# A two-layer convolution block: the order of stores, loads and projections in its first stage, and buffers for its last pieces

## The chip, the cores and the metric

The kernel runs on one core of a Trainium2 chip. The metric is the device time of one execution in microseconds, from the first to the last instruction. All data are float32.

A core has a matrix engine (TensorE), which writes its results into the accumulator memory PSUM; a vector engine (VectorE); a scalar engine (ScalarE), which applies functions and scales; and GpSimd. Each of them works through its own queue of instructions in order. Transfers between the chip's main memory and the on-chip memory are issued here by SyncE (SP in the profile), which does nothing else, by GpSimd (POOL), and at the very end by ScalarE. An issue waits in its queue until what it depends on is done, and everything behind it in that queue waits with it.

## The reference, cut to what matters

The input x has 16 images of 192 channels and 64 by 64 pixels.

```python
# layer 0
h = layernorm_over_channels(x)                     # per pixel
projected, gate = split(conv1x1(h, in_proj))       # 192 -> 2 * 192 channels
projected = depthwise3x3(projected, dw_k)
scanned = weighted sum of four running averages of projected (left, right, down, up)
mixed = (scanned + depthwise3x3(projected, le_k)) * sigmoid(gate)
mixed = gelu(batchnorm(mixed))                     # statistics over all images and pixels
x = x + conv1x1(mixed, out_proj)
x = x + conv1x1(gelu(conv1x1(layernorm(x), fc1)), fc2)   # 192 -> 768 -> 192
# layer 1
t = relu(bn(mean_over_pixels(x) @ w1.T))           # per image
taps = t @ w2.T + b2                               # 3x3 taps per image and channel, masked to 4
out = depthwise3x3(x, taps) + bias
```

The batch norm needs the statistics of all images before its output can be used, so the kernel can't run image by image from end to end.

## The kernel before

Three stages follow each other.

**First stage (L454 to L584): normalise and project.** A pair of images is taken together, one on each half of the 128 partitions. The pixels are cut into n_ac = 64 chunks of 4 groups (AR = 4) of 128 pixels for each of the two images. Four chunks make a block (`per` = 4), and there are 16 blocks. For chunk n:

- `load_a(n)` loads the pixels into one of four xa buffers: six transfers of 128 KB, three on SyncE's queue and three on GpSimd's.
- `turn(n)` transposes them on TensorE into the PSUM tile ps_xt, of which there is one, so that VectorE can take the variance over channels (`variance`, L491 and L492, once for each group). `deviation(n)` takes the root on ScalarE and the reciprocal on VectorE.
- `project(n)` multiplies the raw pixels by the projection weights wi, from which the mean over channels was subtracted (`projection_weights`, in three steps: scale on VectorE, mean on TensorE at L281, subtract on VectorE at L284). Each group fills two PSUM tiles ps_pj, each kept twice. VectorE (L517) and ScalarE (L518) evict one each and multiply it by the reciprocal deviation.
- The evictions write into the block's staging buffer: stg for even blocks, a part of mid for odd ones. So a buffer comes round every second block, and the first eviction of a block waits until the block two before has been stored.

The store of a block is spread over the four iterations of the next block: at its first iteration `store_first` (four transfers of 64 KB) and two parts of `store` (four of 64 KB and four of 448 KB), then one part in each iteration, four transfers of 448, 320 and 192 KB. They lie half on SyncE's queue and half on GpSimd's.

Before the change, iteration n of the loop at L564 puts first `load_a(n + 3)` into the queues, then the stores. The load takes the buffer of chunk n - 1, so it waits for the last matmul of project(n - 1). Then come turn(n + 1), project(n) with the variances of chunk n + 1 among its groups, deviation(n + 1), and the small work that `beside` has set down for this iteration: decay tables, bias rows, their stores to main memory (lv_d, dv_d), and from iteration 40 on the loads of weights and of the first matrices for the second stage (`load_dm`, `load_lm`).

**Second stage: convolution as matrices, scans, gate.** It goes over the channels in 24 groups and reads what the first stage stored. The change leaves it alone.

**Third stage: the rest of layer 0, and layer 1.** It goes over n_ch = 64 chunks of 512 pixels of each image of a pair. Layer 1 of a pair (`dynamic`, 12 pieces of 128 by 1024) is spread over the chunks of the next pair. The last pair has no next one; its twelve pieces come at the end, in `dynamic_last`, in the order of L1109 to L1121. Five of them are done by ScalarE (first tap, L1029) and VectorE (the other three taps, L65 called from L1031). Seven are done on TensorE with the taps on diagonals of small matrices (L1038) and evicted by ScalarE (L1040). All twelve take their output buffer from the ring gl, which has four buffers and was also used by the hidden layer.

The order of instructions on every engine is the order of the program text.

Of the kernel before, what the change touches and what calls it, by code (L numbers as in the profile page):

```python
# [21 lines left out]
F32 = mybir.dt.float32  # L22
# [6 lines left out]
HW = 64  # L29
NPIX = HW * HW  # L30
RW = HW + 2
CH = 512
# [3 lines left out]
GR = 2 * CR  # L36
# [8 lines left out]
AR = CR // 2  # L45
# [10 lines left out]
def conv_block_kernel(ctx: ExitStack, tc: tile.TileContext, x, prm, w_in, w_out, w_fc1, b_fc1, w_fc2, w1, bn1, w2, out):  # L56
# [189 lines left out]
    with ExitStack() as stage:  # L246
# [8 lines left out]
        dg = cut(64, 768, 576).rearrange("p (t k n) -> p t k n", t=3, k=3)  # L255
# [16 lines left out]
        def projection_weights():  # L272

            by_group = lambda v: v.rearrange("p (k g c) -> p g k c", k=2, c=GC)
            flat = lambda v: v.rearrange("p g k c -> p (g k c)")
            for t in range(3):
                nc.vector.tensor_scalar_mul(wi[:, t], by_group(w0[:, t]), pt3[:, t, LN1W:LN1W + 1])
            yield
            pc = bank()
            for t in range(3):  # L280
                nc.tensor.matmul(pc[:, 0:2 * C], mean_w, flat(wi[lo, t]), start=(t == 0), stop=(t == 2))  # L281
            yield
            for t in range(3):
                nc.vector.tensor_sub(flat(wi[:, t]), flat(wi[:, t]), pc[:, 0:2 * C])  # L284
            yield

        def decays():

            nc.scalar.activation(dec, pt3[lo, :, DEC:DEC + 4], AF.Sigmoid)
            nc.vector.tensor_scalar(dec, dec, 0.05, 0.995, ALU.max, ALU.min)  # L290
            nc.scalar.activation(tmp, pt3[lo, :, ISC:ISC + 4], AF.Tanh)
            nc.vector.tensor_scalar_add(tmp, tmp, 1.0)
            nc.vector.tensor_reduce(red, pt3[lo, :, MIX:MIX + 4], AX.X, ALU.max)
            for t in range(3):
                nc.vector.tensor_scalar(gain[:, t], pt3[lo, t, MIX:MIX + 4], red[:, t:t + 1], None, ALU.subtract)
            nc.scalar.activation(gain, gain, AF.Exp)
# [125 lines left out]
        def beside(n, f, *args):  # L422
            side.setdefault(n, []).append((f, args))
# [21 lines left out]
                beside(end + 1 + part, store_vector, k, part)  # L445
        for k in (0, 1, 3, 4):
            beside(40 + k, load_weights, k)
        beside(46, load_dm, 0)
        beside(47, load_lm, 0)
        beside(48, load_dm, 1)  # L450
        beside(49, load_lm, 1)
        beside(50, squeeze_scale)

        xp = stage.enter_context(tc.tile_pool(name="xa", bufs=4))  # L454
# [4 lines left out]
        n_ac = n_pairs * NCH  # L459
# [4 lines left out]
        stag = {}  # L464

        def load_a(n):
            blk, part = divmod(n, per)
            p, u = divmod(blk, 2)
            xa = xp.tile([128, 3, CH], F32, tag="xa", name="xa")
            for i, q in enumerate(HALF):  # L470
                for t in range(3):
                    (nc.sync, nc.gpsimd)[i].dma_start(  # L472
                        xa[q, t].rearrange("p (g n) -> p g n", n=128), xr[2 * p + i, u, :, t, part * AR:(part + 1) * AR])
            ast[n]["xa"] = xa

        def pixels(n, t, g):
            return ast[n]["xa"][:, t, g * 128:(g + 1) * 128]

        def turn(n):

            xt = psa.tile([128, 3, AR, 128], F32, tag="xt", name="ps_xt")
            for t in range(3):
                for g in range(AR):
                    nc.tensor.transpose(xt[:, t, g], pixels(n, t, g), ident)  # L484
            ast[n].update(xt=xt, st6=sp.tile([128, AR, 2, 6], F32, tag="st6", name="st6"),
                          mv=sp.tile([128, AR, 2, 2], F32, tag="mva", name="mva"))

        def variance(n, g):
            s = ast[n]
            for i, q in enumerate(HALF):  # L490
                nc.vector.bn_stats(s["st6"][:, g, i], s["xt"][:, :, g, q])  # L491
                nc.vector.bn_aggr(s["mv"][:, g, i], s["st6"][:, g, i])  # L492

        def deviation(n):
            rs = sp.tile([128, AR, 2], F32, tag="rsa", name="rsa")
            nc.scalar.activation(rs, ast[n]["mv"][:, :, :, 1], AF.Sqrt, bias=eps6)
            nc.vector.reciprocal(rs, rs)
            ast[n]["rs"] = rs

        def project(n):  # L500
            blk, part = divmod(n, per)
            if part == 0:
                if blk % 2:
                    both_i = mid.rearrange("p (i o j) -> p i o j", i=2, j=BR)
                else:
                    both_i = stg.tile([128, 2, 2 * C, BR], F32, tag="stg", name="stg")
                stag[blk] = [both_i[:, i] for i in range(2)]
            for g in range(AR):
                ps = [psa.tile([128, 2 * C], F32, tag=f"pj{i}", name=f"ps_pj{i}", bufs=2) for i in range(2)]
                for t in range(3):  # L510
                    for i, q in enumerate(HALF):
                        nc.tensor.matmul(ps[i], pixels(n, t, g)[q], wi[q, t].rearrange("p g k c -> p (g k c)"),  # L512
                                         start=(t == 0), stop=(t == 2))
                if n + 1 < n_ac:
                    variance(n + 1, g)
                j, rs = part * AR + g, ast[n]["rs"]
                nc.vector.tensor_scalar_mul(stag[blk][0][:, :, j], ps[0], rs[:, g, 0:1])  # L517
                nc.scalar.activation(stag[blk][1][:, :, j], ps[1], AF.Copy, scale=rs[:, g, 1:2])  # L518
# [21 lines left out]
        for dst, src in ((pt3, prm), (w0, w_in)):  # L540
            v = src.rearrange("(t p) n -> p t n", p=64)
# [12 lines left out]
        steps = projection_weights()  # L554
        next(steps)
        decays()
        turn(0)
        next(steps)
        for g in range(AR):
            variance(0, g)  # L560
        next(steps)
        deviation(0)

        for n in range(n_ac):  # L564
            if n + 3 < n_ac:
                load_a(n + 3)
            blk, part = divmod(n, per)
            if blk:
                if part == 0:
                    store_first(blk - 1)  # L570
                    store(blk - 1, 0, (nc.gpsimd, nc.sync))
                store(blk - 1, part + 1, (nc.gpsimd, nc.sync))
                if part == per - 1:
                    stag.pop(blk - 1)
            if n + 1 < n_ac:
                turn(n + 1)
            project(n)
            if n + 1 < n_ac:
                deviation(n + 1)
            for f, args in side.pop(n, ()):  # L580
                f(*args)
# [5 lines left out]
    with ExitStack() as stage:  # L587
# [163 lines left out]
        for k in range(-2, n_bp + 1):  # L751
            if 0 <= k + 1 < n_bp:
                tables(k + 1)
            if k >= 1:
                vertical(k - 1)
                gate(k - 1)
                g, c = divmod(k, hp_)
# [57 lines left out]
    hp2 = ctx.enter_context(tc.tile_pool(name="h2", bufs=2))  # L815
    wp = ctx.enter_context(tc.tile_pool(name="w2", bufs=1))
    op = ctx.enter_context(tc.tile_pool(name="o2", bufs=2))
# [202 lines left out]
    def dynamic_last(p, g, t, dg, queues=(nc.gpsimd, nc.sync)):  # L1020

        xi, taps, r = ximg[p % n_img], pst[p]["taps"], g * GR
        o = wp.tile([128, GR, HW], F32, tag="gl", name="ol", bufs=4)
        src = lambda k, r0, nr: xi[:, t, r0 + k // 3:r0 + k // 3 + nr, k % 3:k % 3 + HW]
        if dg is None:
            for k in range(NTAP):
                w = taps[:, t, k:k + 1]
                if k == 0:
                    nc.scalar.activation(o, src(k, r, GR), AF.Identity, bias=pt3[:, t, BIAS:BIAS + 1], scale=w)  # L1029
                else:  # L1030
                    stt(o, src(k, r, GR), w, o)  # L1031
        else:

            ps = ps2.tile([128, 2, CH], F32, tag="f1", name="ps_d", bufs=2)
            for k in range(NTAP):
                for i, q in enumerate(HALF):
                    for h in range(2):
                        nc.tensor.matmul(rows(ps[HALF[h], i]), dg[q, k, q], src(k, r + h * CR, CR)[q],  # L1038
                                         start=(k == 0), stop=(k == NTAP - 1))
            nc.scalar.activation(o.rearrange("p h w -> p (h w)"), ps.rearrange("p k n -> p (k n)"), AF.Identity,  # L1040
                                 bias=pt3[:, t, BIAS:BIAS + 1])
        for i in range(2):
            if dg is None:
                nc.sync.dma_start(ov[2 * p + i, 64 * t:64 * t + 64, r * HW:(r + GR) * HW], o[HALF[i]].rearrange("p h w -> p (h w)"))
            for h in range(2 if dg is not None else 0):
                r0 = r + h * CR
                queues[h].dma_start(ov[2 * p + i, 64 * t:64 * t + 64, r0 * HW:(r0 + CR) * HW],
                                                  o[HALF[h], i * CR:(i + 1) * CR].rearrange("p h w -> p (h w)"))
# [115 lines left out]
```

## Time and profile before

| | us |
|---|---|
| time, median of 3 runs (lowest to highest) | 3752.0 (3748.82 to 3752.39) |
| span of the profiled execution | 3750.8 |
| TensorE busy | 3696.1 |
| VectorE busy | 2716.6 |
| ScalarE busy | 1794.8 |
| GpSimd busy | 420.2 |
| first matmul of project(0) | 21.93 |
| last matmul of project(63) ends | 633.5 |
| second stage, about | 640 to 1360 |
| taps of the last pair are there, the twelve pieces begin | 3714.85 |

The profile page gives busy times and counts, then the span in 40 equal slices of 94 us, where a digit is the busy share in tenths. A line of the timeline has the start, the duration, engine and line, operation, out<-in with shapes, and in brackets the idle time of the engine before it and what ended that. What ended it is inferred: where several transfers land close together, another of them may be named. On SyncE a line's duration is the time in which its queue was held by the issue.

### The profile page before, as it was taken

Reading aid. Unit: us, or ns where it says so; the run is one execution under the profiler, and the core shown is the slowest. Engines: PE = TensorE matmul, PEld = TensorE weight load, DVE = VectorE, ACT = ScalarE, POOL = GpSimd, SP = SyncE. Lnnn points to the kernel's source line nnn. Section 1 sums busy time; section 2 is a strip of 40 time slices with the busy share of each in tenths; the row PEclk is TensorE's granted clock in tenths of the full one; section 3 lists DMA queues with packets and bytes.
Section 4 is the critical chain, followed back from the end, with each engine's and each line's share of the span. In section 5 each row is a group of like instructions: output and inputs, shape, how many; then the busy total and the mean of one; then the engine's idle time right before and its main releaser. Section 6 shows DMA issues by size and latency. Waiting matters only on the chain.

```text
span 3750.8 us, 71230 instructions
## 1 busy us (share of the span) xinstructions
PE 3696.1 (99%) x30252; PEld 1651.4 (44%) x30252; DVE 2716.6 (72%) x4260; ACT 1794.8 (48%) x1945; POOL 420.2 (11%) x683
## 2 busy tenths in 40 slices
PE   8999999999999979999999999999999999999998
PEld 5666666555555533333333333333333333333333
DVE  6887776999999965557756766666766776675763
ACT  3443434888888833334443434443443434443432
POOL 2334332101001020000000000000000000000000
PEclk9999999999999989999999999999999999999999
DMA  6899998999999950112222222222222221221212
GB/s 163 241 251 235 269 283 249 294 281 277 274 283 269 242 104 18 56 39 71 72 62 66 62 68 64 67 57 68 76 61 55 78 71 40 80 76 43 68 37 74
DMA packets 308429, 491.76 MB, mean 131 GB/s; under 512 B 46656, under 2 KB 202640, under 8 KB 308112
## 3 DMA queue, kind: packets, MB, share of 16 engines
q1 hardware_dynamic: 250064, 295.14, 29.7%
q0 software_dynamic: 57152, 190.94, 18.9%
q8 instruction: 239, 3.92, 0.5%
q10 hardware_dynamic: 896, 1.12, 0.1%
q14 instruction: 78, 0.64, 0.1%
HBM read 284.91 MB, written 197.92 MB: 129 GB/s over the span
## 4 chain that ended last, share of the span: by engine, by line
PE 97%; DVE 1%; DMA 1%; ACT 0%; issue 0%; SPq 0%; ACTq 0%; POOL 0%; DVEq 0%
PE ps_f L955 27%; PE ps_f L828 26%; PE ps_pj L512 13%; PE ps_l L662 11%; PE ps_d L618 7%; PE ps_o L887 5%; PE ps_xt L484 2%; PE ps_o L883 2%; PE ps_o L916 2%; DMA xa<-in_x_dram 1%; PE ps_k L828 0%; DVE v L653 0%; DVE v L655 0%; DMA out_dram<-ol 0%; PE ps_d L1038 0%
## 5 line engine op out<-in xcount | busy, mean ns | idle before, releaser
L957 ACT ACTIVATE gl<-ps_f,bf 128x1024 f32<-128x1024 f32 x384 | 427.6, 1114 | 1316.3 <-PE ps_f L955 1316.3
L955 PE MATMUL ps_f<-h,wf 64*64 64x512 f32 x9216 | 1035.9, 595 | 6.8 <-DVE h L943 6.7
L828 PE MATMUL ps_f<-gl,place 128*64 128x512 f32 x4608 | 1022.2, 592 | 0.0
L955 PEld LDWEIGHTS ps_f<-h,wf 64*64 64x64 f32 x9216 | 334.5, 133 | 693.8 <-issue 642.6
L828 PEld LDWEIGHTS ps_f<-gl,place 128*64 128x64 f32 x4608 | 334.2, 137 | 574.5 <-issue 533.4
L512 PE MATMUL ps_pj<-wi,xa 64*128 64x384 f32 x3072 | 513.8, 487 | 4.0 <-DVE stg L517 3.9
L923 DVE TENSOR_TENSOR h<-ximg,ps_o 128x768 f32<-128x768 f32 x128 | 116.4, 951 | 425.5 <-PE ps_o L887 417.2
L512 PEld LDWEIGHTS ps_pj<-wi,xa 64*128 64x128 f32 x3072 | 292.2, 187 | 197.7 <-issue 10.7
L893 DVE SCALAR_TENSOR_TENSOR ximg<-ps_o,pt,low 128x256 f32<-128x256 f32 x384 | 168.0, 480 | 267.5 <-PE ps_o L887 264.9
L65 DVE SCALAR_TENSOR_TENSOR o<-ximg,taps,o 128x1024 f32<-128x1024 f32 x252 | 323.2, 1282 | 8.7 <-ACT o L1014 2.6
L1018 POOL DMA_DIRECT2D out_dram<-o x168 | 87.9, 528 | 2067.6 <-DVE o L65 2064.8
L942 DVE RECIPROCAL rs<-rs 128x512 f32<-128x512 f32 x64 | 214.3, 3349 | 27.0 <-ACT rs L939 27.0
L653 DVE TENSOR_TENSOR_SCAN v<-tab,q 128x1024 f32<-128x1024 f32 x96 | 218.3, 2274 | 7.8 <-ACT tab L641 7.8
L655 DVE TENSOR_TENSOR_SCAN v<-tab,q 128x1024 f32<-128x1024 f32 x96 | 217.5, 2265 | 0.0
L887 PE MATMUL ps_o<-low,wo 128*64 128x256 f32 x1536 | 210.2, 395 | 0.0
L518 ACT ACTIVATE stg<-ps_pj,rsa 128x384 f32<-128x384 f32 x128 | 119.8, 940 | 187.9 <-PE ps_pj L512 177.0
L641 ACT ACTIVATE tab<-mask,dec_b 128x1024 f32<-128x1024 f32 x192 | 209.0, 1137 | 0.0
L518 ACT ACTIVATE mid<-ps_pj,rsa 128x384 f32<-128x384 f32 x128 | 120.6, 943 | 181.6 <-PE ps_pj L512 175.0
L491 DVE BATCH_NORM_STATS2 st<-ps_xt 128x6 f32<-128x192 f32 x512 | 173.2, 338 | 17.1 <-PE ps_xt L484 16.9
L239 DVE STREAM_TRANSPOSE low<-low 128x512 f32<-128x512 f32 x174 | 167.6, 1014 | 2.1 <-issue 0.3
L975 DVE SCALAR_TENSOR_TENSOR ximg<-ps_f,pt,ximg 128x512 f32<-128x512 f32 x192 | 134.4, 749 | 40.2 <-PE ps_f L828 37.8
L472 POOL DMA_DIRECT2D xa<-in_x_dram x192 | 119.8, 630 | 357.8 <-PE ps_pj L512 279.3
(197 smaller groups left out, 4101.9 us busy)
## 6 DMA issues: line engine op xcount, KB each, us to landing
low<-in_x_dram SPq DMA_DIRECT2D x128, 384.0 KB
out_dram<-o POOLq DMA_DIRECT2D x168, 256.0 KB, 3.7
mid<-pg_d SPq DMA_DIRECT2D x8, 4096.0 KB
low<-mixed_d SPq DMA_DIRECT2D x116, 256.0 KB
low<-pg_d SPq DMA_DIRECT2D x7, 4096.0 KB
pg_o<-pg_d SPq DMA_DIRECT2D x7, 4096.0 KB
xa<-in_x_dram POOLq DMA_DIRECT2D x192, 128.0 KB, 5.9
xa<-in_x_dram SPq DMA_DIRECT2D x192, 128.0 KB
```

The lines of the kernel that those rows point to most:

```text
L65: nc.vector.scalar_tensor_tensor(o, in0, scalar, in1, ALU.mult, ALU.add, **kw)
L512: nc.tensor.matmul(ps[i], pixels(n, t, g)[q], wi[q, t].rearrange("p g k c -> p (g k c)"), start=(t == 0), stop=(t == 2))
L518: nc.scalar.activation(stag[blk][1][:, :, j], ps[1], AF.Copy, scale=rs[:, g, 1:2])
L618: nc.tensor.matmul(dst(ps[o, ih]), mats[g % 2]["dm"][q, di + 1, :, ch], src(s["pg"][q, :, 0, ch]), start=(di == 0), stop=stop)
L653: nc.vector.tensor_tensor_scan(vf, tab, q, 0.0, ALU.mult, ALU.add)
L655: nc.vector.tensor_tensor_scan(vf[:, ::-1], tab[:, ::-1], q[:, ::-1], 0.0, ALU.mult, ALU.add)
L662: nc.tensor.matmul(dst(bst[k]["ps"][i][o]), lm_of(g)[q, m, :, c], src(q, ih), start=start, stop=stop)
L828: nc.tensor.matmul(ps[q], w(i), rhs(i), start=start, stop=stop)
L887: nc.tensor.matmul(ps[q, wh].rearrange("p (r w) -> p r w", w=32), wo[:, 64 * t:64 * t + 64], cols(rows(s["mx"][:, i]))[:, :, wh], start=Fa ...
L942: nc.vector.reciprocal(rs, rs)
L955: nc.tensor.matmul(pf[o, i], wf1[q, t, m0:m0 + 64], s["h"][q, t], start=(t == 0), stop=(t == 2))
L957: nc.scalar.activation(gl, pf, AF.Gelu, bias=bf1[:, m:m + 1])
```

## The change

There are four edits.

1. **Stores ahead of the load.** In iteration n the stores of the block before go into the queues first, and `load_a(n + 3)` after them. They are meant to leave as soon as their data is there, and not to stand behind a load that waits for a buffer.
2. **Matrix loads spread.** The four loads of the second stage's first matrices were set down for iterations 46, 47, 48 and 49; now load_dm is at 46 and 50, load_lm at 48 and 52. This is meant to take them out of the way of stores and x loads.
3. **Projection ahead of transposes, at the start.** The three steps of `projection_weights` are done before the first transposes. In iteration 0 the first two groups are projected before turn(1), and the variances of chunk 1 follow two at a time in the other two groups. All later iterations keep their order. TensorE is meant to begin sooner.
4. **Own output buffers for VectorE's pieces at the end.** The five pieces that VectorE does take their output from the ring o (two buffers, for g below 2, three pieces) and from the ring h2 (two buffers, for the other two), both unused by then. The ring gl is left to the seven pieces of TensorE.

```diff
-        beside(46, load_dm, 0)
-        beside(47, load_lm, 0)
-        beside(48, load_dm, 1)
-        beside(49, load_lm, 1)
+        for i in range(2):
+            beside(46 + 4 * i, load_dm, i)
+            beside(48 + 4 * i, load_lm, i)
...
-        def project(n):
+        def project(n, groups, beside_it):
+
             blk, part = divmod(n, per)
-            if part == 0:
+            if blk not in stag:
...
-            for g in range(AR):
+            for g in groups:
...
-                if n + 1 < n_ac:
-                    variance(n + 1, g)
+                for v in beside_it(g) if n + 1 < n_ac else ():
+                    variance(n + 1, v)
...
         decays()
+        next(steps)
+        next(steps)
         turn(0)
-        next(steps)
         for g in range(AR):
             variance(0, g)
-        next(steps)
         deviation(0)
 
         for n in range(n_ac):
-            if n + 3 < n_ac:
-                load_a(n + 3)
             blk, part = divmod(n, per)
             if blk:
...
                 store(blk - 1, part + 1, (nc.gpsimd, nc.sync))
...
+            if n + 3 < n_ac:
+                load_a(n + 3)
+
+            h = AR // 2 if n == 0 else 0
+            project(n, range(h), lambda g: ())
             if n + 1 < n_ac:
                 turn(n + 1)
-            project(n)
+            project(n, range(h, AR), lambda g: (g,) if h == 0 else (2 * (g - h), 2 * (g - h) + 1))
...
     def dynamic_last(p, g, t, dg, queues=(nc.gpsimd, nc.sync)):
...
-        o = wp.tile([128, GR, HW], F32, tag="gl", name="ol", bufs=4)
+        if dg is None:
+            o = (op.tile([128, GR, HW], F32, tag="o", name="o") if g < 2 else
+                 hp2.tile([128, 3, CH], F32, tag="h2", name="ol")[:, 0:2].rearrange("p k (h w) -> p (k h) w", w=HW))
+        else:
+            o = wp.tile([128, GR, HW], F32, tag="gl", name="ol", bufs=4)
```

## The prediction

> **What bounds the kernel now.** I read the page's busy shares first, then TensorE's waits, then the stretches in which TensorE is idle.
>
> ```profile
> PE 3696.1 (99%) x30252; PEld 1651.4 (44%) x30252; DVE 2716.6 (72%) x4260; ACT 1794.8 (48%) x1945; POOL 420.2 (11%) x683
> PE   8999999999999979999999999999999999999998
> DMA  6899998999999950112222222222222221221212
> ```
>
> TensorE is busy for 3696.1 of 3750.8 us, so all its idle time is 54.7 us, and no edit here takes a matmul away. By stretch: 11.85 us lie in the first 20 us, 5.0 in the rest of the first stage, 25.6 between 700 and 1390, 12.4 in the last 51. The third is a stage that VectorE fills (661.4 of 690 us) and that the edits don't touch; it only starts earlier or later. So the change works on about 29 us.
>
> The first stage, by stretch (us, then TensorE, its weight loads, VectorE, ScalarE, GpSimd busy, clock, DMA share, GB/s):
>
> ```profile
> 20.00:270.00 250.00, 249.95 (x1619) 159.09 (x1619) 200.53 (x660) 98.55 (x132) 88.16 (x148) 1.00 0.82 220
> 270.00:560.00 290.00, 286.08 (x1824) 177.92 (x1821) 216.77 (x642) 115.81 (x155) 114.73 (x191) 1.00 0.99 263
> ```
>
> TensorE sets the pace, 9.40 us a chunk, and from 270 to 560 us the DMA engines are full beside it. There it loses 3.92 us, in two stalls (timeline of TensorE, then of ScalarE and SyncE, round the longer one):
>
> ```profile
> 330.54 4.14 PE L512 MATMUL ps_pj<-wi,xa 64*128 64x384 f32 x24
> 337.21 4.14 PE L512 MATMUL ps_pj<-wi,xa 64*128 64x384 f32 x24 [2.54 <-DVE stg L517]
> ```
> ```profile
> 336.18 1.58 ACT L518 ACTIVATE stg<-ps_pj,rsa 128x384 f32<-128x384 f32 x2 [6.13 <-DMA low<-mid]
> ```
> ```profile
> 310.98 11.96 SPq L472 DMA_DIRECT2D xa<-in_x_dram  x3
> 322.98 2.12 SPq L536 DMA_DIRECT2D pg_d<-stg  x2
> 325.27 3.26 SPq L472 DMA_DIRECT2D xa<-in_x_dram  x3
> 328.57 1.25 SPq L536 DMA_DIRECT2D pg_d<-stg  x2
> ```
>
> Chunk 32 opens a block and writes into stg. ScalarE and VectorE wait for a DMA; what holds that buffer is the last store of the block two before. SyncE issued it at 328.57, behind an x load that waits for project of chunk 30 to give its buffer back. TensorE stops once both PSUM buffers are full. The same happens at 488.6 (1.38 us).
>
> The x loads had time to spare (tile xa, issue to landing):
>
> ```profile
> DMA to landing us min/median/max: 3.1/5.9/11.2
> ```
>
> A load issued at the start of iteration n is wanted by turn(n+3), two chunks on, 18.8 us: typically 12.9 us spare.
>
> The end:
>
> ```profile
> 3728.92 1.11 ACT L1040 ACTIVATE ol<-ps_d,pt 128x1024 f32<-128x1024 f32 x1 [2.51 <-DMA out_dram<-ol]
> 3735.77 1.24 ACT L1029 ACTIVATE ol<-ximg,pt,taps 128x1024 f32<-128x1024 f32 x1 [2.99 <-DVE ol L65]
> 3744.62 1.11 ACT L1040 ACTIVATE ol<-ps_d,pt 128x1024 f32<-128x1024 f32 x1 [3.45 <-DMA out_dram<-ol]
> ```
>
> Twelve pieces go through four gl buffers; from the fifth on ScalarE waits until a store has landed.
>
> [...]SyncE's and GpSimd's transfers together give the 0.99. [...]the store stands behind the waiting load. [...]Here twelve transposes take 2.82 us at 19.18 and 1.53 later; if they switched from 3.26 (three fours of 1.09) to 1.53, the switch fell near 21.6, 7.6 us after work became continuous at 14.03. [...]and I use 7.6.
>
> **Part 1, the start.** Before: transposes wait for x until 14.03, the mean matmuls run 15.04 to 19.2 (4.21), turn(1) to 21.9, project(0) from 21.93, project(1) from 31.33.
> After: VectorE has wi at 9.55 (8.47 + 1.08), so the mean matmuls fill the wait: 9.6 to 13.8. turn(0) has its first two thirds of x by then (they started at 11.47 at the latest) and its last at 14.0: three times 1.09, to 17.1. VectorE subtracts by 15.3 (1.48), hidden by turn(0). Two groups of project(0) follow at once, 4.0 us (half of 8.01), to 21.1; their results wait in PSUM. VectorE's variance(0) takes 3.84 (15.15 to 18.99 before), 17.1 to 20.95, so turn(1) may overwrite xt at 21.1 (1.5, to 22.6). The deviation is there at 21.55, and two evictions of 0.9 end at 23.35. Groups 2 and 3 end at 26.6.
> Now VectorE is last: four variances of 1.02 and two evictions of 0.9 from 23.35, with the fourth variance ahead of the last eviction, end the reads of xt at 28.35. turn(2) waits for that, and project(1) starts at 29.9 instead of 31.33: **-1.4 us**. Bounds: -3.1 if VectorE didn't hold turn(2); +2.4 if the first two groups still ran at half rate.
>
> **Part 2, stores ahead of loads, matrix loads spread.** Bytes by the issue sizes: a block of four chunks stores 2.36, 1.83, 1.31 and 0.79 MB in its four iterations and loads 0.79 MB in each: 9.44 MB in 37.6 us, 251 GB/s, where 263 were moved when full. I count 265 and take the DMA as one line, from a block's start:
> - Last store. Before, it can't be issued until 28.2 (its load waits), and the 9.44 MB end at 36; the first write into that buffer comes 2.1 us into the next block at 39.7. Spare: 4 us, which the lag round chunk 32 exceeded by 2.5. After, it goes one chunk sooner and one load fewer lies ahead: 8.65 MB, plus 1.0 for the last eviction, 33.6. Spare: 6.
> - First load. After, it stands behind 2.36 MB and the wait for the last eviction (VectorE ends 30.9 where the matmuls ended 29.9): 3.15 MB are 11.9, plus 1.0, 12.9 of the 18.8 us. Spare: 5.9 instead of 12.9.
> - Second load: 5.77 MB, 21.8 + 1.0 = 22.8, wanted at 28.2. Spare 5.4. The third and fourth have 7 and 10.
> So the smallest spare grows from 4 to 5.4 us, and the load wait that is added (behind it on SyncE and GpSimd are only later stores and small loads; turn waits for it) stays inside it. A lag of 6.5 as round chunk 32 would still leave 1.1 us, but stores issued a chunk sooner fill moments in which the DMA had nothing (share 0.67 and 0.85 from 290 to 298 us: 2 us). Moving three matrix loads one to three iterations later takes 640 KB, 2.5 us, from ahead of the store that stalled at 488.6. I take both stalls as gone, and 0.6 us in which chunk 44 ran long (8.61 for 8.01), less 0.3: **-4.2 us**. Bounds: 0 to -4.5.
>
> **Part 3, the end.** Same instructions, other buffers. VectorE's five pieces leave the gl ring; the seven TensorE pieces have four buffers of their own. Up to 3726.4 nothing changes (VectorE's third piece waits for ScalarE behind a TensorE piece). Then ScalarE no longer waits for stores: the third TensorE piece is ready 3.43 after 3724.17 and evicted at 3727.6, not 3728.92; VectorE's fourth piece starts at 3730.4 without a gap, its fifth at 3734.3 and ends at 3738.2 instead of 3741.0. TensorE does pieces in 3.43 each: 3731.0, 3734.45, 3737.9, 3741.3. The last eviction ends at 3742.4, against 3745.73. The end came 5.07 after that: 3747.5. By bytes: 6.29 MB leave from 3720.2 on; at 225 GB/s that is 3748.1. I take 3747.8: **-3.0 us**. Bounds: 0 (the stores drain no faster) and -4.
>
> **Sum:** -1.4 - 4.2 - 3.0 = -8.6; 3752.0 - 8.6 = 3743.4 us. The other stages move up whole.
>
> **Rivals.**
> A: the load wait takes the stall's place. For: DMA share 0.99, spare halved. Against: DMA is idle in places, and chunks before 270 have room. Part 2 gives nothing: 3752.0 - 4.4 = 3747.6. Chance 0.22.
> B: the end is bound by bytes, part 3 gives 0.5: 3752.0 - 6.1 = 3745.9. For: share 0.78 and 221 GB/s from 3725 to 3750. Against: 263 when full. Chance 0.13.
> C, slower: the loads run late in every block from 270 to 560 us, seven or eight blocks at 2 us, +15, since a late x load stops TensorE and VectorE both; 3752.0 + 15 - 4.4 = 3762.6. For: chunk 32's load had only 5.0 us spare before. Against: the bytes fit. Chance 0.06.
> Main case 0.59.
>
> **How the numbers follow.** The 0.2% bound is 7.5 us, 3744.5. Of the main case some three quarters lie below it, of A none, of B a third, and a start better than computed adds a little: faster 0.54. Slower is C and its neighbours: 0.07. The rest, 0.39, is within. For 8 in 10 the range reaches from 3738.5 (start -3.1, part 2 whole, end -4, and 2 us between runs) past A to 3750.5.
>
> **What would show it.** Mean matmuls first, at 9.6, and project(1) near 29.9. No waits for stg or mid at chunks 32, 44, 48. A spare of 5 to 6 us at the x loads of each block's first iteration, no wait of ps_xt for xa after the start. In the end, no ScalarE wait for out_dram, VectorE without a gap after 3730. Wrong if ps_xt waits for xa at 320 to 330, if the first groups run at half rate, or if the last stores land as late as before.

## The result, and the profile after

The changed kernel takes 3788.6 us (median of 4 runs, 3783.9 to 3794.7) where the kernel before takes 3751.05 (4 runs). The ratio is 1.0102, 95% interval 1.0082 to 1.0121: it is 1% slower. The forecast was 3743.4 us.

From the timelines of both profiles the span can be cut at four instructions:

| us | before | after | difference |
|---|---|---|---|
| start to the first matmul of project(1) | 31.3 | 28.8 | -2.6 |
| from there to the end of project(63) | 602.2 | 638.4 | **+36.2** |
| second and third stage, to the taps of the last pair | 3081.2 | 3081.3 | +0.1 |
| the twelve last pieces | 36.1 | 33.7 | -2.4 |

Start and end gained what they should, near enough. All of the loss lies in the steady part of the first stage: of its 36.2 us, 25.9 are idle time of TensorE (4.0 us before, 29.9 after) and 10.3 are longer busy time (598.2 and 608.5). First the page's slices of the changed kernel (TensorE, DMA):

```profile
PE 3706.0 (98%) x30252; PEld 1664.7 (44%) x30252; DVE 2717.1 (72%) x4260; ACT 1795.1 (47%) x1945; POOL 420.3 (11%) x683
PE   8999999999999979999999999999999999999998
DMA  6899987999999961112222222222221221221212
```

The slices hardly show it. TensorE is even busy for 9.9 us more, with the same 30252 instructions. What TensorE waited for, first before (all three waits lie at the start, while the first x arrives), then in the changed kernel, longest first:

```profile
PE ps_xt L484 <- DMA xa<-in_x_dram: 11.9, 3, 9.6
```

```profile
PE ps_xt L483 <- DMA xa<-in_x_dram: 21.5, 20, 3.0
PE pb L281 <- DVE wi L277: 9.0, 1, 9.0
...
PE ps_xt L483 <- DVE rsa L496: 2.8, 2, 1.4
PE ps_xt L483 <- DVE wf L397: 2.0, 1, 2.0
...
PE ps_xt L483 <- DMA pg_d<-mid: 1.3, 1, 1.3
```

No wait for stg or mid by ps_pj is left; the transposes (ps_xt) wait for x instead. The lines that name VectorE or a store are taken for the same wait, put down to whatever came last: nothing that they name is read by a transpose. With the smaller ones it is some 29 us. By stretch:

```profile
20.00:270.00 250.00, 243.06 (x1577) 153.91 (x1575) 196.45 (x648) 96.73 (x131) 87.83 (x148) 1.00 0.80 212
270.00:560.00 290.00, 272.93 (x1705) 169.02 (x1703) 202.24 (x597) 108.48 (x145) 108.58 (x181) 0.98 0.91 245
```

In the second line TensorE idles for 17 us where it idled for 4, and the DMA engines, full before, now have room (0.91 for 0.99), which fits a TensorE that is late and so frees the buffers late.

One block, first SyncE's queue (the second number is the time for which the issues held it), then TensorE:

```profile
547.14 1.16 SPq L530 DMA_DIRECT2D low<-stg  x2
548.35 2.66 SPq L536 DMA_DIRECT2D pg_d<-stg  x4
551.19 7.08 SPq L471 DMA_DIRECT2D xa<-in_x_dram  x3
```
```profile
556.97 8.01 PE L512 MATMUL ps_pj<-wi,xa 64*128 64x384 f32 x48
566.71 0.63 PE L483 MATMUL ps_xt<-ident,xa 128*128 128x128 f32 x4 [1.73 <-DMA xa<-in_x_dram]
569.12 1.08 PE L483 MATMUL ps_xt<-ident,xa 128*128 128x128 f32 x4 [1.78 <-DMA xa<-in_x_dram]
570.41 1.09 PE L483 MATMUL ps_xt<-ident,xa 128*128 128x128 f32 x4 [0.21 <-DMA pg_d<-stg]
571.43 9.53 PE L512 MATMUL ps_pj<-wi,xa 64*128 64x384 f32 x48
```

Project of chunk 51 ended at 546.2, and with that the block's first iteration began. SyncE issued six stores, then the three loads that are its half of chunk 55 (one of the two images). It was held by them till 558.3. TensorE wanted chunk 55 at 565.0, and its three thirds came so late that the transposes ended at 571.5. The granted clock fell too: four transposes take 1.09 and not 0.51, and the next project 9.53 and not 8.01. The trace's record of the granted clock stands at one half from 567.7 to 574.5, and three more times in the steady part, 20.5 us in all; before, it never does there. At half the rate these 20.5 us do the work of 10, which accounts for the 9.9 us of busy time.

How x loads fare, in the trace of the packets, counted from the end of the project that frees the buffer (medians over the blocks; turn wants them at 18.8):

| SyncE's half, block's first iteration | before | after |
|---|---|---|
| issue begins | 0.1 | 5.1 |
| first packet of the load moves | 1.5 | 12.4 |
| last packet lands | 5.8 | 20.6 |
| moved until then by GpSimd's queue, MB | 0.48 | 3.14 |
| moved until then by SyncE's queue, MB | 0.48 | 1.93 |

GpSimd's half is issued at 4.4 and lands 10.8 later, at 15.2: in time.

The end, on ScalarE:

```profile
3761.39 1.11 ACT L1047 ACTIVATE ol<-ps_d,pt 128x1024 f32<-128x1024 f32 x1 [1.19 <-PE ps_d L1045]
3762.40 1.23 ACT L1036 ACTIVATE ol<-ximg,pt,taps 128x1024 f32<-128x1024 f32 x1
...
3776.05 1.11 ACT L1047 ACTIVATE ol<-ps_d,pt 128x1024 f32<-128x1024 f32 x1 [3.30 <-DMA out_dram<-ol]
```

From the third TensorE piece on ScalarE waits for TensorE and no longer for a store; only the last piece waits about 1 us for a buffer (TensorE had it at 3775.0).

### The profile page after: what moved, and what is told of

It reads as the page before. It is cut to its first block, busy times and chain, and to the rows that moved or that the text cites. A ratio compares the mean times of both kernels' runs of the same rounds, so it can differ in the third digit from the quotient of the medians.

```text
span 3782.1 us, 71222 instructions
## 1 busy us (share of the span) xinstructions
PE 3706.0 (98%) x30252; PEld 1664.7 (44%) x30252; DVE 2717.1 (72%) x4260; ACT 1795.1 (47%) x1945; POOL 420.3 (11%) x683
## 4 chain that ended last, share of the span: by engine, by line
PE 91%; DMA 6%; DVE 1%; issue 1%; SPq 1%; POOL 0%; ACT 0%; POOLq 0%; DVEq 0%; ACTq 0%
PE ps_f L958 27%; PE ps_f L831 26%; PE ps_l L665 11%; PE ps_pj L512 9%; PE ps_d L621 7%; PE ps_o L890 5%; DMA xa<-in_x_dram 4%; PE ps_o L886 2%; PE ps_xt L483 2%; PE ps_o L919 1%; PE ps_d L1045 0%; SPq L471 0%; DMA ximg<-mixed_d 0%; PE ps_k L831 0%; DVE v L656 0%
## 5 line engine op out<-in xcount | busy, mean ns | idle before, releaser
L831 PEld LDWEIGHTS ps_f<-gl,place 128*64 128x64 f32 x4608 | 334.2, 137 | 574.5 <-issue 533.4
L65 DVE SCALAR_TENSOR_TENSOR o<-ximg,taps,o 128x1024 f32<-128x1024 f32 x261 | 334.7, 1282 | 9.3 <-ACT o L1017 2.6
L517 DVE TENSOR_SCALAR mid<-ps_pj,rsa 128x384 f32<-128x384 f32 x128 | 115.3, 901 | 52.0 <-PE ps_pj L512 50.5
```

The costliest lines, as they stand in the source:

```text
L65: nc.vector.scalar_tensor_tensor(o, in0, scalar, in1, ALU.mult, ALU.add, **kw)
L831: nc.tensor.matmul(ps[q], w(i), rhs(i), start=start, stop=stop)
```

## The experiments

The first theory was that SyncE's half of the x load is late because it stands behind the block's stores in its queue. The rivals: the DMA engines have no room for any order that serves stores sooner; or the other edits cost the time. On the chips of these runs the kernel before took 3758 to 3763 us, so ratios to it are compared.

**All edits but the first.** In the changed kernel:

```diff
         for n in range(n_ac):
+            if n + 3 < n_ac:
+                load_a(n + 3)
             blk, part = divmod(n, per)
...
-            if n + 3 < n_ac:
-                load_a(n + 3)
```

> All edits but the first: the x load stands ahead of the stores again, as before the change. Theory (the x load of a block's first iteration comes late because it stands behind that block's stores on SyncE's queue): the loss in the first stage is gone, the start keeps 2.5 us, the end 2.4 us, the spread matrix loads up to 1.4 us: 3743 to 3747 us. Rival 1 (the DMA engines have no room, each gain of a store is a load's loss): the same here. Rival 2 (the loss comes from the spread matrix loads, or from the new start): 3770 us or more.

Ratio 0.9977 (0.9968 to 0.9987). The other edits are a gain, and rival 2 is out. In its profile project(1) starts at 27.4 (31.3 before) and the last pieces take 34.3 (36.1).

**The first edit alone**, on the kernel before: `load_a(n + 3)` moved behind the stores.

> The kernel before with the first edit alone, stores ahead of the x load. Theory and rival 1: all of the loss of the first stage, some 36 us, without the gains of start and end: 3780 to 3793 us, with waits of the transposes for xa at the fourth chunk of most blocks. Rival 2: no loss, 3745 to 3752 us.

Ratio 1.0117 (1.0094 to 1.0140), which is 44 us of 3760. The first edit makes the whole loss, and somewhat more than the 36 us; no run separates what the difference comes from. TensorE's first wait in this run:

```profile
PE ps_xt L484 <- DMA xa<-in_x_dram: 54.0, 24, 9.3
```

**Load first in a block's first iteration.**

```diff
+            if part == 0 and n + 3 < n_ac:
+                load_a(n + 3)
             if blk:
...
-            if n + 3 < n_ac:
+            if part and n + 3 < n_ac:
                 load_a(n + 3)
```

> The changed kernel, but in the first iteration of a block (where 2.36 MB of stores go out) the x load goes ahead of the stores; in the other three iterations the stores stay ahead. Theory: no wait for xa, and the stalls for the staging buffer stay away, since the block's last store still leaves a chunk sooner: 3741 to 3746 us. Rival 1: the lateness moves to the loads of the second and third iteration, 3760 us or more. Rival 2: unchanged, about 3788 us.

Ratio 1.0005 (0.9995 to 1.0016): most of the loss is gone, but the expected gain didn't come. The lateness moved to the next load. SyncE's half for the block's second iteration is issued 5.5 after the buffer is free and lands 13.2 after that, at 18.7. Here rival 1 was half right: not only the first iteration's stores are too many to stand ahead.

```profile
PE ps_xt L483 <- DMA xa<-in_x_dram: 19.7, 12, 3.6
```

**Queues apart.** In the changed kernel all x loads go to GpSimd and all stores of the loop to SyncE:

```diff
-                    (nc.sync, nc.gpsimd)[i].dma_start(
+                    nc.gpsimd.dma_start(
                         xa[q, t]...
...
-                (nc.gpsimd, nc.sync)[par].dma_start(pg_even...
+                nc.sync.dma_start(pg_even...
...
-                    store(blk - 1, 0, (nc.gpsimd, nc.sync))
-                store(blk - 1, part + 1, (nc.gpsimd, nc.sync))
+                    store(blk - 1, 0, (nc.sync, nc.sync))
+                store(blk - 1, part + 1, (nc.sync, nc.sync))
```

> The changed kernel with all x loads issued by GpSimd and all stores of the loop by SyncE: neither stands behind the other in a queue, the bytes are the same. Theory: x loads land within about 10 us of their issue, no waits for xa, 3741 to 3747 us. Rival 1: the DMA engines are as full as in the changed kernel, loads are late as there, 3765 us or more. Rival 2: about 3788 us.

Ratio 0.9962 (0.9949 to 0.9975): 14 us less than before on the same chip. It is the lowest ratio of the study, though its interval overlaps that of the kernel with the load ahead (0.9968 to 0.9987). The same bytes fit well, so rival 1 in its plain form is out. TensorE's waits and GpSimd's queue:

```profile
PE pb L281 <- DVE wi L277: 9.1, 1, 9.1
PE ps_pj L512 <- DVE stg L517: 3.3, 1, 3.3
```
```profile
538.38 3.67 POOL L471 DMA_DIRECT2D xa<-in_x_dram  x6 [5.73 <-PE ps_pj L512]
547.78 3.65 POOL L471 DMA_DIRECT2D xa<-in_x_dram  x6 [5.73 <-PE ps_pj L512]
```

All six loads are issued within 4.0 us of the buffer's release, every 9.4 us, and no transpose waits for x in the steady part. But one stall for stg is there (chunk 32), and the steady part takes 602.3 us, as before (602.2): what this kernel gains lies outside it, most of it at the start (3.2 us) and the end (2.7).

**Queues apart, the other way.** But is it the place in the queue, or the queue? In the packets of the trace SyncE's x loads are 49,152 packets of 512 bytes, one for each run of x. GpSimd's queue has 160 of that size in all; its loads go in packets of 4096, and the bytes of the stores on both queues mostly in packets of 3 to 7 KB. My guess, theory packets, is that a load in small packets moves slowly beside stores in large ones. The traces so far don't show that, but it can be tried. The mirror: all x loads on SyncE, all stores of the loop on GpSimd (the diff above with the names exchanged).

> The mirror of the kernel with queues apart: all x loads issued by SyncE, all stores of the loop by GpSimd. Nothing stands behind the other here either. Theory place (only the place in the queue counts): as with the queues the other way, 0.996 of before, 3741 to 3748 us on a chip where before takes 3752. Theory packets (SyncE's x loads go in packets of 512 bytes, GpSimd's stores in packets of several KB, [...]so that the loads crawl until the stores are out): x loads land 15 us or more after their issue in a block's first iterations, waits for xa, 1.005 of before or more.

Ratio 1.0062 (1.0047 to 1.0077). No load stands behind a store in either kernel, and yet they lie 1.0% apart, so theory place alone is out. The second iteration's load lands 18.4 after its issue (10.8 with GpSimd), and its issue holds SyncE for 10.2. The first iteration's load, which starts before the stores, lands in 6.9.

```profile
PE ps_xt L483 <- DMA xa<-in_x_dram: 31.0, 14, 5.8
```

**SyncE's half issued by ScalarE**, in the changed kernel:

```diff
-                    (nc.sync, nc.gpsimd)[i].dma_start(
+                    (nc.scalar, nc.gpsimd)[i].dma_start(
```

> The changed kernel, but the half of each x load that SyncE issued is issued by ScalarE, whose queue holds no stores. Theory place: that half lands within about 8 us of its issue and the loss is gone, 3742 to 3752 us where before takes 3752 (ScalarE's own issues, 2 us a chunk, are beside its 40% of work). Theory packets: the loads, still in packets of 512 bytes, crawl beside the stores of two queues, and at least half of the loss of 36 us stays: 3765 us or more.

Ratio 1.0293 (1.0268 to 1.0317), but this doesn't answer the question as meant. The issues themselves held ScalarE, which should have evicted:

```profile
460.41 6.57 ACTq L471 DMA_DIRECT2D xa<-in_x_dram  x2
467.08 1.57 ACT L518 ACTIVATE mid<-ps_pj,rsa 128x384 f32<-128x384 f32 x2 [10.59 <-DMA pg_d<-stg]
```

TensorE waited 91 us for ScalarE's evictions. One number counts against the place alone: the second iteration's half, with no store in its queue at all, still landed 17.3 after its issue, though its three issues themselves were held for some 10 of these.

**Load first on one queue only.** `load_a` takes a list of halves; in the changed kernel one half goes ahead of the stores and the other stays behind them.

```diff
         for n in range(n_ac):
+            if n + 3 < n_ac:
+                load_a(n + 3, (0,))      # the other run: (1,)
...
             if n + 3 < n_ac:
-                load_a(n + 3)
+                load_a(n + 3, (1,))      # the other run: (0,)
```

First SyncE's half ahead:

> The changed kernel with the x load ahead of the stores on SyncE's queue alone; GpSimd keeps stores ahead of the load. Theory (it is SyncE's half that comes late): the loss is gone but for a us or two, ratio to before 0.997 to 1.001. Rival (GpSimd's half or the bytes as a whole): 1.006 or more.

Then GpSimd's half ahead:

> The reverse: the x load ahead of the stores on GpSimd's queue, stores ahead of it on SyncE's. Theory (SyncE's half comes late): most of the loss stays, ratio 1.006 to 1.014. Rival (GpSimd's half, or the bytes as a whole): 0.997 to 1.002, or half of the loss.

Ratios 0.9990 (0.9983 to 0.9997) and 1.0009 (1.0001 to 1.0017). TensorE's waits for x, in the same order:

```profile
PE ps_xt L484 <- DMA xa<-in_x_dram: 9.2, 3, 4.2
```
```profile
PE ps_xt L484 <- DMA xa<-in_x_dram: 13.8, 9, 4.2
```

The first is as expected. The second is not, and lies where the rival put it: SyncE's half still stands behind SyncE's stores, and three quarters of the loss are gone all the same. In that run GpSimd's stores of the next iteration stand behind its own next load, which waits for a buffer. GpSimd's queue moves 2.01 MB before SyncE's half lands, and not 3.14, and that half lands at 15.9, not 20.6. So the lateness on SyncE is made in good part by what GpSimd's queue moves meanwhile.

**Longer runs of x.** To change the length of the runs of x, and with it the packets on SyncE, and leave the places in the queues (the pixels then reach other places of the output, so these three kernels serve for times alone):

```diff
-        xr = x.rearrange("b (t p) (j u r) w -> b u p t j (r w)", p=64, u=2, r=2)
+        xr = x.rearrange("b (t p) (u j r) w -> b u p t j (r w)", p=64, u=2, r=2)
```

In the changed kernel:

> The changed kernel with x read in runs of 2048 bytes and not 512: a block takes 32 successive pixel rows and not every other pair of rows, so the pixels reach the output in another order; the bytes, the transfers and their places in the queues are the same. Theory packets [...]: SyncE's half lands several us sooner, three quarters of the loss are gone, ratio to before 0.996 to 1.001. Rival place and bytes: the loss stays, 1.007 or more.

In the kernel with all loads on SyncE:

> All x loads on SyncE, all stores of the loop on GpSimd, and x in runs of 2048 bytes (pixels in another order, as in the run beside it). Theory packets: loads land in about half of the 18.4 us after issue that the worst ones took with 512 bytes; ratio 0.995 to 1.000. Rival place and bytes: as with 512 bytes, 1.005 to 1.008.

In the kernel with the load ahead:

> The control for the two: the x load ahead of the stores as before the change, the other edits kept, and x in runs of 2048 bytes (pixels in another order). Both theories: TensorE sets the pace there already, so no more than the stalls that were left can go: 0.994 to 0.998, where 512 bytes gave 0.9977.

| ratio to before | runs of 512 bytes | runs of 2048 bytes |
|---|---|---|
| stores ahead (the change) | 1.0102 (1.0082 to 1.0121) | 1.0010 (1.0003 to 1.0016) |
| loads on SyncE, stores on GpSimd | 1.0062 (1.0047 to 1.0077) | 0.9982 (0.9974 to 0.9989) |
| load ahead | 0.9977 (0.9968 to 0.9987) | 0.9966 (0.9952 to 0.9979) |

TensorE's waits for x in the first two (21.5 and 31.0 us with runs of 512 bytes):

```profile
PE ps_xt L483 <- DMA xa<-in_x_dram: 12.7, 12, 3.0
```
```profile
PE ps_xt L483 <- DMA xa<-in_x_dram: 5.1, 3, 3.7
```

The control moves by 0.1%, inside its intervals; the two others gain 0.9 and 0.8%. Against the control two thirds of the change's loss go with the longer runs (0.0125 becomes 0.0044), somewhat less than the three quarters expected. So the length of the runs matters much.

Why the length matters is not shown. The loads became faster by less than expected: SyncE's half of the first load lands at 18.8 and not 20.6, just when it is wanted, and its first packet still moves only at 12.0; on SyncE alone the second iteration's load lands 16.5 after its issue, where about half of 18.4 was expected. The packets can be counted in the two kernels with loads on SyncE and stores on GpSimd, between 100 and 600 us, in those microseconds in which both moved and GpSimd's took at least half of the DMA time. There 105 load packets of 512 bytes went beside 44 of GpSimd's, or 36 of 2048 bytes beside 45. So beside about as many of GpSimd's packets, packets of four times the length carried only a third more bytes. (Whether each queue always had a packet ready the trace doesn't tell.) A packet of 512 bytes took 27 ns there and one of 2048 bytes 84, a fifth less for the same bytes.

**Queues apart, matrices as before**, so edit 2 undone in the kernel with queues apart.

> The kernel with queues apart (loads on GpSimd, stores on SyncE), but the four loads of matrices in iterations 46 to 49 as before the change. If the spreading is worth what the forecast gave it, one stall of 1 to 3 us at chunk 48 comes back: ratio 0.9965 to 0.998 where the spread one gave 0.9962. If it is worth nothing, 0.9955 to 0.9965.

Ratio 0.9968 (0.9955 to 0.9980), against 0.9962 (0.9949 to 0.9975). In its profile the stall at chunk 48 is back (the next chunk starts 5.9 us late) and one at chunk 32, 5.0 in the other profile, is absent. No effect on the time can be told from this.

## Why the prediction was wrong

**Part 1, the start: right, the gain bigger than said.** Forecast -1.4, measured -2.6. TensorE before, then after:

```profile
31.33 8.01 PE L512 MATMUL ps_pj<-wi,xa 64*128 64x384 f32 x48
```
```profile
8.96 4.20 PE L281 MATMUL pb<-wi,wf 64*128 64x384 f32 x6 [8.96 <-DVE wi L277]
13.10 2.82 PE L483 MATMUL ps_xt<-ident,xa 128*128 128x128 f32 x12
15.85 5.27 PE L512 MATMUL ps_pj<-wi,xa 64*128 64x384 f32 x24
...
28.76 8.01 PE L512 MATMUL ps_pj<-wi,xa 64*128 64x384 f32 x48
```

The mean matmuls ran at 8.96 (forecast 9.6) and turn(0) at 13.1 (13.8). The first two groups took 5.27 us, not 4.0. At full rate they take 4.14 (as the other two do at 22.50), at half rate twice that, 8.28, so by estimate the clock was released 2.26 us into them, about 18.1; the record of the granted clock has full rate from 18.2 (and before from 21.9, where the prediction worked out 21.6). That is 9.2 us after work began, and not 7.6. So the sign "if the first groups run at half rate" came true in part. It cost nothing, since VectorE's variances came early too (15.96 for 17.1), and these held turn(2), as forecast (27.3 for 28.35).

**Part 3, the end: right.** Forecast -3.0, measured -2.4. VectorE runs its third and fourth piece without a gap and ends 23.4 us after the taps (forecast 23.5):

```profile
3760.23 7.76 DVE L65 SCALAR_TENSOR_TENSOR ol<-ximg,taps,ol 128x1024 f32<-128x1024 f32 x6 [1.80 <-ACT ol L1036]
```

The last eviction ends 28.75 after them and not 27.7, with the store wait of about 1 us in it.

**Part 2, the stores: right that the waits go, but no gain followed.** In the changed kernel no chunk waits for its staging buffer any more. The 4.2 us that this was to give showed up in no run: the forecast needs a steady part of 598.0 us, and the shortest in any profile is 601.4 (load ahead, long runs; one profile each, on several chips).

**Part 2, the loads: here it failed.** The step was "I count 265 and take the DMA as one line", and from it "3.15 MB are 11.9, plus 1.0, 12.9 of the 18.8 us". The rate was near enough: until SyncE's half landed at 20.6, 5.07 MB had moved in the 19.6 us after the last eviction, 259 GB/s. The line was wrong. There are two queues, each in its own order, and the half that lands last decides. 3.14 MB of the 5.07 were GpSimd's: its stores and its load, then the stores of the next iteration, which the first edit itself lets go without waiting for a buffer, the load behind them, and the first stores of the iteration after. SyncE's queue got 1.93 MB. The load's first packet moved at 12.4 where the sum had the stores out by 9.9, and it took 8.2 to move where the sum had 3.0; before it took 4.3. The mirror run shows that the queue on which a load goes has a large part in that (1.0062 against 0.9962), the long runs that the length of its runs has (1.0010 against 1.0102), and the run with GpSimd's load ahead that GpSimd's early stores have (1.0009). GpSimd's half landed at 15.2, nearer to the sum.

With it fell the claim that the smallest spare grows from 4 to 5.4 us. The loads had 13 us before; the change spent these and more to gain 2 us for a store.

**One line for both queues.** Between 270 and 560 us of the kernel before, SyncE's queue has 0.54 and GpSimd's 0.44 of the DMA share of 0.99. I read the sum as if the issuer made no difference, and that was not shown. These runs differ: the same loads and stores on exchanged queues lie 1.0% apart (0.9962 and 1.0062).

**Rival C was what happened, its size too small.** It had 2 us in seven or eight blocks, between 270 and 560 us, +15. The lateness began near 150 us, TensorE waited for x at 315 to 318 (2.7 us; the prediction's sign was 320 to 330), and the steps to chunks 50 and 54 alone took 5.6 and 5.1 us too long. And it left out the clock: 9.9 us of busy time.

**Still open.** How the DMA engines share their time between a store in packets of 7 KB and a load of 512 bytes, and so why long runs help, stays open. So does the part of the loss that long runs leave (0.0044): the time of the first packet (12.0) points to the place behind the stores, but no experiment separates it.

## What to carry to other kernels

When a transfer is moved behind others, follow each queue by itself, with all that the other queues may send in the same time, and ask for the half that lands last. In this kernel a load with a deadline and short runs fared badly behind and beside large stores that have none: SyncE's half of a block's first load landed at 20.6 us and not 5.8. What helped was a queue each for loads and stores, with the short runs on the queue where they travel in packets of 4096 bytes and not 512 (ratio 0.9962 where the change has 1.0102); or longer runs (1.0010); or leaving the stores behind the load that paces them (0.9977). An order that holds transfers back may look like a waste and be, as here, what keeps the urgent ones fast.

## What the runs showed of the hardware

- The same x, in the same runs of 512 bytes, moved in packets of 512 bytes from SyncE's queue and of 4096 from GpSimd's. With runs of 2048 bytes SyncE's packets had 2048.
- An issue held its engine though the buffer was free: three loads that took 2.0 us to issue elsewhere held SyncE for 7.1, and two held ScalarE for 6.6. What they wait for the traces don't name. ScalarE had evictions behind them, and TensorE waited 91 us for those.
- In the steady part of the changed kernel the granted clock fell to one half four times, each time in a wait of the transposes or just after one. At 567.7, for 6.8 us, it fell in the second of two waits of 1.7 and 1.8 us (four transposes then took 1.08 us for 0.51); at 441.4, for 3.4, in the second of two of 1.4 and 0.9; at 523.3, for 6.8, in one of 3.0; at 318.5, for 3.4, just after one of 2.7. After a single wait of 2.0 us (to 247.7) it stayed at full rate.
